# Four columns of the identity instead of 128 behind a strided operand, and one step more for reloaded inputs

## The chip, the cores and the metric

The kernel runs on one core of one Trainium2 chip. The metric is the device time of one execution in microseconds (us). The kernel before took 3438.81 us (median of 3 runs, 3435.35 to 3440.09); with the run made beside the change it is 3437.78 us (4 runs).

## The reference

A graph attention layer with 8 frames of 2048 nodes, 256 channels and 8 heads of 32, a feed-forward of 256, and three layer norms. All is float32. What matters here is the softmax over masked scores and its denominator.

```
qkv = einsum('fnc,ck->fnk', x, w_qkv)
scores = einsum('fnhd,fmhd->fhnm', q, k) / sqrt(D)
scores = where(adj > 0, scores, -1e9)
attn = softmax(scores)                      # exp / sum of exp
t = einsum('fhnm,fmhd->fnhd', attn, v)
x = layernorm(x + t); h = relu(x @ w1 + b1); x = layernorm(x + h @ w2 + b2)
return layernorm(x_in + x)
```

## The kernel before

The work is a list of 1024 steps: frame f (8), a chunk of 512 queries qc (4), a group g of four heads (2), a block of 128 keys mb (16). A step holds the scores of four heads (line 215, TensorE), the mask (line 218, VectorE, out of PSUM), the exponential (line 222, ScalarE) and the products with the values (line 234, TensorE). At most one bank of side work (projections, feed-forward, turned inputs, sums of exponentials) is put into each step, by generators that say at each `yield` what they wait for: a number of steps, or a bank.

The sums of exponentials of one group, 64 times in all:

```python
def denominator(f, qc, g):
    ...
    for n, term in enumerate(terms):          # sums over keys: ones.T @ term, heads at rows 0,32,64,96
        ...
            nc.tensor.matmul(ps[r:r + D, :], cst["ones"], term[:, h, :], ...)      # L292
    dT = op.tile([P, CH], F32, name="dT")
    nc.scalar.copy(dT, ps)                    # L294: 128 rows (32 equal ones a head) x 512 queries
    yield 1
    yield BANK
    ps = bank()
    for j in range(TPC):                      # four transposes, queries j, j+4, j+8, ...
        nc.tensor.transpose(ps[:, j * P:(j + 1) * P], dT[:, j::TPC], ident)        # L299
    ...
    den = ps.rearrange("p (j c) -> p j c", c=P)[:, :, ::D]      # one of 32 equal columns a head
    nc.vector.reciprocal(rc[:, :, 4 * g:4 * g + 4], den)                           # L304
    nc.vector.tensor_tensor(RS[:, 0], RS[:, 0], den, ALU.add)                      # L305
    nc.vector.tensor_tensor(RS[:, 1], RS[:, 1], den, ALU.min)                      # L306
```

The transposes make 128 columns of which four are read. The load of inputs that were turned before:

```python
def reload(f, c):
    ...
    xT = take([P, 2, CH], F32)
    nc.sync.dma_start(xT, XD[f][c])           # in<-xd
    yield 3                                   # steps until the first product may stand
    return xT

# in the main loop, when a step needs a projection that isn't there yet:
    while (nf, nmb // TPC, ng) not in V:
        advance(t0, 1)                        # runs side work now, and counts steps that don't pass
        t0 += 1
```

## Time and profile before

| | before |
|---|---|
| time, median | 3437.78 us |
| TensorE busy, waiting for VectorE | 3179.1 us, 174.6 us |
| VectorE, ScalarE, GpSimd busy | 2731.0, 2426.5, 2586.7 us |
| sums of exponentials (L299): records, block | 256 loads and 256 moves, 0.68 us |
| mean granted clock | 0.990 |

"Block" is the time from the first start of L299 to the start of the next work of TensorE, read from the starts of single instructions; the timeline shows the same. PE is the matrix products of TensorE and PEld the loads of their stationary operands. The prediction shows the lines and reads them.

### The profile page before, as it was taken

The page shows a single profiled execution, that of the slowest core. Times are in us where ns is not written, and L with a number is a line of the kernel's source. Part 1 is how long each engine was busy: PE and PEld are TensorE (multiplying, and loading weights), DVE is VectorE, ACT ScalarE, POOL GpSimd, SP SyncE. Part 2 cuts the span into 40 slices and gives each one's busy share as a digit, 9 for nine tenths or more (in the row PEclk, how much of TensorE's full clock was granted, in tenths as well). Part 3 has the DMA queues.
Part 4 walks back from the last instruction along what each step waited for, and adds up shares of the span by engine and source line. Part 5 has one row for each costly group of instructions (what it writes and reads, how often), then busy time and mean ns, then how long its engine had stood idle before and what let it go on. Part 6 is the DMA issues. An engine that isn't in the chain of part 4 may idle for free. (4 is left out here: it accounts for less than half of the span.)

```text
span 3439.1 us, 54435 instructions
## 1 busy us (share of the span) xinstructions
PE 3179.1 (92%) x22036; PEld 1038.5 (30%) x22036; DVE 2731.0 (79%) x3203; ACT 2426.5 (71%) x1937; POOL 2586.7 (75%) x1357
## 2 busy tenths in 40 slices
PE   6989999999999999999999999999999999998995
PEld 5222332223322233222332323223332223322222
DVE  4788768887788877888788887888768887689885
ACT  3677767776677767777677776777767777677774
POOL 0577768887688776888678876787777877788885
PEclk8999999999999999999999999999999999999998
DMA  8678768778678777778777777687776787777774
GB/s 309 149 156 173 173 161 174 158 159 200 142 167 184 154 180 153 163 172 181 170 154 170 161 175 178 141 180 172 164 179 140 160 187 167 169 158 154 151 162 99
DMA packets 149298, 575.99 MB, mean 167 GB/s; under 512 B 14608, under 2 KB 67344, under 8 KB 99888
## 3 DMA queue, kind: packets, MB, share of 16 engines
q0 software_dynamic: 64560, 435.85, 63.2%
q1 hardware_dynamic: 83664, 135.30, 11.4%
q8 instruction: 174, 2.85, 0.3%
q10 hardware_dynamic: 816, 1.31, 0.1%
q14 instruction: 84, 0.69, 0.1%
HBM read 131.99 MB, written 37.75 MB: 49 GB/s over the span
## 5 line engine op out<-in xcount | busy, mean ns | idle before, releaser
L218 DVE TENSOR_TENSOR p<-s,mask 128x1024 f32<-128x1024 f32 x2048 | 2410.0, 1219 | 568.5 <-PE s L215 343.9
L222 ACT ACTIVATE p<-p 128x2048 f32<-128x2048 f32 x1024 | 1956.6, 1911 | 484.6 <-DVE p L218 371.2
L256 POOL TENSOR_TENSOR p<-p 128x2048 f32<-128x2048 f32 x382 | 1851.8, 4898 | 385.9 <-ACT p L222 383.4
L215 PE MATMUL s<-qT,kT 32*128 32x512 f32 x8192 | 1169.8, 641 | 184.9 <-DVE p L218 174.6
L234 PE MATMUL x<-p,v 128*32 128x512 f32 x8192 | 1091.8, 605 | 2.3 <-ACT p L222 2.3
L253 POOL DMA_DIRECT2D p<-p x384 | 385.6, 1024 | 376.0 <-DMA p<-p 188.4
L215 PEld LDWEIGHTS s<-qT,kT 32*128 32x128 f32 x8192 | 320.5, 183 | 822.3 <-DVE p L218 756.2
L234 PEld LDWEIGHTS x<-p,v 128*32 128x32 f32 x8192 | 161.1, 108 | 780.1 <-issue 211.5
L172 PE MATMUL x<-in,wqkv 128*128 128x512 f32 x472 | 235.2, 621 | 14.7 <-DMA in<-xd 14.1
L292 PE MATMUL x<-p,ones 128*32 128x512 f32 x2064 | 244.9, 592 | 1.9 <-DMA p<-p 1.9
L274 ACT ACTIVATE y<-y,nb,rs 128x256 f32<-128x256 f32 x372 | 219.0, 590 | 7.1 <-POOL nb L271 7.1
L263 DVE BATCH_NORM_STATS2 st<-y 128x6 f32<-128x256 f32 x372 | 155.4, 418 | 0.0
L172 PEld LDWEIGHTS x<-in,wqkv 128*128 128x128 f32 x472 | 80.2, 189 | 170.9 <-issue 112.7
L294 ACT COPY dT<-x 128x512 f32<-128x512 f32 x64 | 37.4, 585 | 126.3 <-PE x L292 126.3
L415 PE MATMUL x<-w2s,hT 128*128 128x256 f32 x504 | 125.5, 392 | 0.1
L405 PE MATMUL x<-turned,w1s 128*128 128x512 f32 x248 | 123.0, 618 | 0.0
L197 PEld LDWEIGHTS x<-wqkv,in 128*128 128x128 f32 x896 | 104.2, 191 | 47.0 <-issue 41.1
L197 PE MATMUL x<-wqkv,in 128*128 128x128 f32 x896 | 114.9, 281 | 0.0
L292 PEld LDWEIGHTS x<-p,ones 128*32 128x32 f32 x2064 | 66.8, 110 | 156.4 <-issue 151.0
L415 PEld LDWEIGHTS x<-w2s,hT 128*128 128x128 f32 x504 | 90.6, 189 | 62.0 <-issue 50.3
L268 POOL TENSOR_TENSOR rs<-rs,mhalf 128x4 f32<-128x4 f32 x93 | 96.2, 1035 | 7.8
L200 ACT COPY v<-x 128x512 f32<-128x512 f32 x58 | 33.9, 585 | 93.6 <-PE x L197 93.6
(114 smaller groups left out, 1467.6 us busy)
## 6 DMA issues: line engine op xcount, KB each, us to landing
p<-p POOLq DMA_DIRECT2D x384, 1024.0 KB, 10.1
mask<-md SPq DMA_DIRECT2D x248, 128.0 KB, 6.2
y<-in_x_dram POOLq DMA_DIRECT2D x62, 512.0 KB, 6.1
in<-xd SPq DMA_DIRECT2D x59, 512.0 KB, 10.9
p<-in_adj_dram SPq DMA_DIRECT2D x16, 1024.0 KB, 9.6
out_dram<-y SPq DMA_DIRECT2D x31, 512.0 KB, 6.4
in<-in_x_dram SPq DMA_DIRECT2D x29, 512.0 KB, 10.4
xd<-in SPq DMA_DIRECT2D x28, 512.0 KB, 9.2
```

Source lines behind the costliest of these rows:

```text
L172: nc.tensor.matmul(ps, wqkv[:, a, k0:k0 + P], xT[:, a, :], start=(a == 0), stop=(a == 1))
L197: nc.tensor.matmul(ps[:, j * P:(j + 1) * P], xT[:, a, j * P:(j + 1) * P], wqkv[:, a, 2 * C + g * P:2 * C + (g + 1) * P], start=(a == 0), s ...
L215: nc.tensor.matmul(ps2[half][:, j, :], KT[f, mb // TPC, g][r:r + D, (mb % TPC) * P:(mb % TPC + 1) * P], QT[f, qc, g][r:r + D, :], start=Tr ...
L218: nc.vector.tensor_tensor(pt[:, 2 * half:2 * half + 2, :], ps, MK[f, qc, mb // 2][:, mb % 2, None, :].to_broadcast([P, 2, CH]), ALU.add)
L222: nc.scalar.activation(PT[item], PT[item], AF.Exp, scale=1.0 / math.sqrt(D))
L234: nc.tensor.matmul(O[grp][r:r + D, :], V[f, mb // TPC, g][:, mb % TPC, r:r + D], PT[item][:, h, :], start=(mb == 0), stop=(mb == LAST))
L253: nc.gpsimd.dma_start(PT[f, qc, g, chain[0]], PT.pop(item), accum_op=ALU.add)
L256: nc.gpsimd.tensor_tensor(first, first, PT.pop(item), ALU.add)
L263: nc.vector.bn_stats(st, t[:, j, :])
L274: nc.scalar.activation(t[:, j, :], t[:, j, :], AF.Identity, bias=nb[:, j:j + 1], scale=rs[:, j:j + 1])
L292: nc.tensor.matmul(ps[r:r + D, :], cst["ones"], term[:, h, :], start=(n == 0), stop=(n == len(terms) - 1))
L415: nc.tensor.matmul(ps[:, (j - jj) * C:(j - jj + 1) * C], hT[:, d, j * P:(j + 1) * P], w2s[:, d, :], start=(d == 0), stop=(d == 1))
```

## The change

Of each transpose's 128 columns only four are used. The change makes them alone: a true product with four columns of the identity (0, 32, 64, 96) as the moving operand, in the hope of a shorter block on the busiest engine. The second part lets the first product with a reloaded input stand one step later, in the hope that its load has landed by then.

```diff
         nc.sync.dma_start(xT, XD[f][c])
-        yield 3
+        yield 4
         return xT
...
-            nc.tensor.transpose(ps[:, j * P:(j + 1) * P], dT[:, j::TPC], ident)
+            nc.tensor.matmul(ps[:, 4 * j:4 * j + 4], dT[:, j::TPC], ident[:, ::D], start=True, stop=True)
...
-        den = ps.rearrange("p (j c) -> p j c", c=P)[:, :, ::D]
+        den = ps[:, 0:4 * TPC].rearrange("p (j h) -> p j h", h=4)
```

## The prediction

> **What bounds the kernel now.** I read the page first (busy times, the 40 slices), then the waits of TensorE, then the timeline around single sums of exponentials (the page calls them L299), then the durations line by line.
>
> The page's busy times, and the granted clock over the span:
>
> ```profile
> PE 3179.1 (92%) x22036; PEld 1038.5 (30%) x22036; DVE 2731.0 (79%) x3203; ACT 2426.5 (71%) x1937; POOL 2586.7 (75%) x1357
> ...
> PEclk8999999999999999999999999999999999999998
> ```
>
> TensorE is busy 92% at a full clock, the others 71 to 79%. The waits of TensorE say how much is left to it:
>
> ```profile
> PE s L215 <- DVE p L218: 174.6, 359, 1.5
> PE x L172 <- DMA in<-xd: 14.1, 8, 3.1
> ```
>
> Only 174.6 us of 3439 go to waiting until VectorE has freed a score bank, and 14.1 us in 8 waits to the loads of turned inputs. So TensorE bounds most steps, and VectorE the rest. There are 1024 steps. In each, the scores take 1.07 us of TensorE (start of L215 to start of L234 in the timeline below), the values 1.00, and a step may hold one bank of side work: 0.59 to 1.98. VectorE needs 2.36 us a step for the mask alone, plus its own side work. A step with no side work or a short one is VectorE's, one with a long one (1.9 us) is TensorE's. One sum of exponentials, in the timeline:
>
> ```profile
> 1450.55 1.06 PE L234 MATMUL x<-p,v 128*32 128x512 f32 x8
> 1450.74 2.35 DVE L218 TENSOR_TENSOR p<-s,mask 128x1024 f32<-128x1024 f32 x2 [0.86 <-PE s L215]
> 1451.54 0.56 PEld L299 LDWEIGHTS x<-ident,dT 128*128 128x128 f32 x4 [0.84 <-issue]
> 1451.54 0.75 PE L299 MATMUL x<-ident,dT 128*128 128x128 f32 x4
> 1452.22 0.31 PEld L215 LDWEIGHTS s<-qT,kT 32*128 32x128 f32 x8
> 1452.22 1.14 PE L215 MATMUL s<-qT,kT 32*128 32x512 f32 x8
> ...
> 1453.56 0.23 DVE L304 RECIPROCAL rc<-x 128x16 f32<-128x16 f32 x1
> ...
> 1453.73 0.16 DVE L306 TENSOR_TENSOR RS<-RS,x 128x16 f32<-128x16 f32 x1
> 1453.81 2.35 DVE L218 TENSOR_TENSOR p<-s,mask 128x1024 f32<-128x1024 f32 x2
> ```
>
> The reader is to see two things. The four transposes hold TensorE from 1451.54 to 1452.22, 0.68 us. And VectorE has no idle time from 1450.74 on (no bracket of its own after that): the scores it uses at 1453.81 ended at 1452.22 + 1.14 = 1453.36, so TensorE has a margin of 0.45 us in this step.
>
> [...] a float32 product is two records (L215 has 8192 for 4096 calls)[...]. A float32 transpose is one record (L299: 256 for 64 x 4 calls). [...] Below, a plain load takes 186 ns for 128 columns and 80 for 2: a slope of 0.84 ns a column[...] on some 79 ns of latency. [...] The transposed operand here has a step of exactly 16 bytes (every fourth float32), and its loads take 213 ns against 141 for the same transpose with contiguous operands (L394). [...] The only products of one column here (L741) start 27 ns apart (0.19 us for two records of at most 165 ns).
>
> **The change part by part.** The diff replaces a transpose by a true product with four moving columns. The columns fall from 128 to 4, but what is loaded, dT in 128 strided columns, stays, and a product is two records where a transpose was one. So each block goes from 4 loads and 4 moves to 8 loads and 8 moves. The durations by line (min/median/max in ns):
>
> ```profile
> L299 PEld LDWEIGHTS x<-ident,dT x252: 195/213/221, 159.0 to 3352.5; 128*128 128x128 f32 x126
> L299 PE MATMUL x<-ident,dT x252: 283/286/386, 159.0 to 3352.6; 128*128 128x128 f32 x126
> ```
> ```profile
> L394 PEld LDWEIGHTS x<-ident,y x256: 137/141/230, 265.9 to 3406.4; 128*128 128x128 f32 x128
> ```
> ```profile
> L197 PEld LDWEIGHTS x<-wqkv,in x896: 186/192/192, 312.2 to 3010.6; 128*128 128x128 f32 x180
> ```
> ```profile
> L741 PEld LDWEIGHTS okp<-ones,ok x2: 80/82/83, 3412.3 to 3412.3; 128*2 128x2 f32 x2
> L741 PE MATMUL okp<-ones,ok x2: 163/164/165, 3412.3 to 3412.3; 128*2 128x1 f32 x2
> ```
>
> Now: four transposes, whose starts in the trace are 0.22, 0.12 and 0.12 us apart, then 0.21 until the next block starts: 0.68. In the trace a move starts 109 ns after its load where operands are contiguous (L197, 128 columns) and 120 where they are strided (L299), and the next load starts only then. So in L197, one record each 112 ns, the move's own 107 ns hide behind the load already; taking them away gains nothing. After: about 0.11 to the first move, 7 more at 0.12 each, and 0.10 from the last move to the next block (the 0.21 of now less 0.107 of streaming): 0.11 + 0.84 + 0.10 = 1.05 us. The block gets **0.37 us longer** (an estimate from these starts), times 64 = 24 us of TensorE.
>
> How much of it reaches the end? I listed, for each of the 64 sums, TensorE's waits in the steps after it while VectorE is busy without a gap. In 16 sums of the second group a bank of 0.79 us of waiting follows, after two of 0.11: nothing gets through. In 7 others, 0.11 + 0.11 + 0.20: nothing. In 7, 0.22 in all, then a long side block: 0.15 each, 1.1 us. In 19 of the first group 0.34 (two turned blocks): 0.03 each, 0.6 us. In 4 of the last frame over 0.7: nothing. In 9 of the first group a projection of 1.9 us follows at once, and no wait for 20 us or more: all of it, 9 x 0.37 = 3.3 us. The two left, the first frame's and the very last, which stands in the chain to the end: 0.7. Sum: **5.7 us**.
>
> VectorE's part is the same work: 16 elements from contiguous instead of strided places, in 0.23, 0.11 and 0.16 us.
>
> The second part, one step more between a load of turned inputs and its first product: the order of instructions differs in one place only, six query products near 104 us, each one step later. No load waits there; the 8 waits of 14.1 us are later, in projections that are forced when scores need them, and the order leaves those alone. So it is worth nothing: 0 +- 1 us.
>
> **The rivals.** *A: fewer columns, less time.* If a load hid behind other work, a record would cost the 27 ns of L741, 8 x 0.027 + 0.2 = 0.4 us a block, 0.27 less. Against it: L741 loads 2 columns, not 128, and the pace of L197. And the same waits that hide a loss hide a gain: only some 9 to 18 sums would give it, 3 to 5 us: 3434. *B: strided plain loads at half speed.* Strided transposes load in about 98 ns (start of first to start of second load) against 56 contiguous. If plain loads doubled likewise, from 107 to 200 or more, the block would be 8 x 0.21 + 0.2 = 1.9 us, 1.2 longer, over VectorE's margin of 0.45: about 0.75 x 64 = 48 us at the end: 3487. For it: no plain strided load exists in this trace. Against it: a plain load takes only one column per 0.84 ns, and a strided transpose load reads one per 0.9 (115 ns over 126 columns), so the memory gives what a plain load needs. *C: VectorE or the loads become the bound.* Nothing of theirs changes, the order of DMA issues is the same.
>
> **Range and chances.** 3438.8 + 5.7 = 3444.5, said as 3445. My main case (some 78%) covers 3440 to 3450 with the scatter of the runs before (3435 to 3440); A (8%) gives 3432 to 3437; B (14%) 3460 to 3490. The range, 8 in 10: 3437 to 3462. Over 2% means below 3371 or above 3509: TensorE's whole 64 blocks are 64 x 0.68 = 44 us, 1.3%, so faster is all but out; slower needs B without any hiding (77 us).
>
> **What would show it.** 512 moves and 512 loads on L299 in place of 256; starts of its moves about 0.12 us apart; 1.05 us from its start to the next block; the loads at 190 to 215 ns; the waits of TensorE for VectorE down by about 18 us of their 174.6; the reload waits still 8 and about 14 us. Wrong if the records come closer than 0.1 us (A), or at 0.2 (B), or if the reload waits go.

The 107 ns that the prediction takes for a move of 128 columns is an estimate from the starts in the trace of before: records of 512 columns (L172, L405) follow each other in 429 ns, of which 107 is a quarter, and records of 256 (L415) in 216, so some 0.83 ns a column. The 3, 13, 53 and 107 ns of streaming in the expectations below are the same estimate for 4, 16, 64 and 128 columns.

## The result

The changed kernel took 3537.06 us (median of 4, 3534.58 to 3542.05), 99 us more. The ratio is 1.0291 (95% interval 1.0273 to 1.0309). Ratios here are the mean time of one kernel's fast runs over that of the other's of the same rounds, so not quite the ratio of the medians. The prediction's range ended at 3462.

The page of the changed kernel, its waits of TensorE, and the durations of its L299:

```profile
PE 3305.2 (93%) x22292; PEld 1135.7 (32%) x22292; DVE 2745.6 (78%) x3203; ACT 2428.3 (69%) x1937; POOL 2588.0 (73%) x1357
```
```profile
PE s L215 <- DVE p L218: 160.5, 355, 1.4
...
PE x L172 <- DMA in<-xd: 10.4, 6, 2.6
```
```profile
L299 PEld LDWEIGHTS x<-ident,dT x504: 307/329/332, 157.9 to 3451.4; 128*128 128x128 f32 x168
L299 PE MATMUL x<-ident,dT x504: 374/374/397, 157.9 to 3451.4; 128*128 128x4 f32 x168
```

All the other engines do the same work; TensorE has 256 products and 256 loads more, as predicted. But a load takes 329 ns, where I expected 190 to 215. The timeline of one sum, the same one that the prediction shows of before, with the step that follows:

```profile
1486.63 1.06 PE L234 MATMUL x<-p,v 128*32 128x512 f32 x8
1486.82 2.36 DVE L218 TENSOR_TENSOR p<-s,mask 128x1024 f32<-128x1024 f32 x2 [0.86 <-PE s L215]
1487.62 1.94 PEld L299 LDWEIGHTS x<-ident,dT 128*128 128x128 f32 x8 [0.84 <-issue]
...
1489.59 1.97 PE L215 MATMUL s<-qT,kT 32*128 32x512 f32 x8
...
1491.48 1.88 PE L234 MATMUL x<-p,v 128*32 128x512 f32 x8
...
1491.60 2.35 DVE L218 TENSOR_TENSOR p<-s,mask 128x1024 f32<-128x1024 f32 x2 [1.55 <-PE s L215]
...
1493.98 1.14 PE L215 MATMUL s<-qT,kT 32*128 32x512 f32 x8
```

Two things are to be seen. The block runs from 1487.62 to 1489.59, **1.96 us** where it was 0.68 (all but the last of the 64 blocks have this length). And the scores and values right after it take 1.97 and 1.88 us, where before, and again at 1493.98, they take 1.14 and 1.06. The busy times by stretch (length, then busy time and count of PE, PEld, DVE, ACT, POOL, the granted clock, DMA) say why:

```profile
1486.40:1489.80 3.40, 3.40 (x24) 2.32 (x24) 2.94 (x5) 2.22 (x2) 1.00 (x2) 1.00 0.94 193
1489.80:1493.20 3.40, 3.40 (x16) 0.38 (x12) 1.85 (x5) 1.38 (x1) 3.13 (x5) 0.50 0.95 193
1493.20:1496.60 3.40, 3.40 (x28) 1.59 (x24) 2.86 (x4) 1.91 (x1) 3.01 (x1) 1.00 1.11 231
```

For one window of 3.41 us the granted clock is 0.50. PE is "busy" for all of each stretch; only the clock tells. The page's 40 slices of 88 us do not show such windows, their digit stays 9. The mean over the whole run does, and is the first thing I should have looked at in the result; here before and after:

```profile
core 0: 3439.1 us, clock 0.990
```
```profile
core 0: 3537.2 us, clock 0.974
```

From the clock's records between the first sum and the end I counted the halved windows that begin within 4 us of a block's start: 35 of the 64 blocks in the changed kernel, none of before. (The long halved stretches near the end, 7 us and more, which every kernel here has, are left out, here and below.) Each of the 35 is 3.41 us long, and they lie on a grid of 3.41 us. All blocks that start 0.13 to 1.34 us after a grid line (32), or at most 0.08 us before one (3), have the clock halved in the next window; of the 29 that start elsewhere none has. Those 35 are the blocks whose loads, some 1.9 us long, lie inside one window, wholly or but for the first 0.08 us.

**Where the 99 us lie.** The order of the steps is the same, so I compared the start of the k-th scores in both traces. Across each of the 29 sums without a halved window the kernel falls back by 0.90 us on average; across each of the 35 with one, by 2.07. That is 64 x 0.90 = 58 us for the longer blocks and 35 x 1.17 = 41 us for the clock, 99 in all. This is bookkeeping on one pair of traces; the experiments test it.

### The profile page after: what moved, and what is told of

The parts are those of the page before. It is cut to its first block, busy times and chain, and to the rows that moved or that the text cites. A ratio compares the mean times of both kernels' runs of the same rounds, so it can differ in the third digit from the quotient of the medians.

```text
span 3537.2 us, 54947 instructions
## 1 busy us (share of the span) xinstructions
PE 3305.2 (93%) x22292; PEld 1135.7 (32%) x22292; DVE 2745.6 (78%) x3203; ACT 2428.3 (69%) x1937; POOL 2588.0 (73%) x1357
## 4 chain that ended last, share of the span: by engine, by line
PE 72%; DVE 15%; DMA 4%; issue 4%; POOL 2%; ACT 1%; DVEq 0%; SPq 0%; ACTq 0%; POOLq 0%
PE s L215 27%; PE x L234 17%; DVE p L218 14%; PE x L292 6%; PE x L172 6%; PE x L299 3%; PE x L415 3%; PE x L405 3%; PE x L197 3%; DMA in<-xd 2%; DMA p<-p 1%; PE x L394 1%; PE x L152 1%; DMA xd<-in 1%; POOL p L256 1%
## 5 line engine op out<-in xcount | busy, mean ns | idle before, releaser
L215 PE MATMUL s<-qT,kT 32*128 32x512 f32 x8192 | 1185.7, 649 | 163.1 <-DVE p L218 160.5
L234 PE MATMUL x<-p,v 128*32 128x512 f32 x8192 | 1120.4, 620 | 1.5 <-ACT p L222 1.5
L172 PE MATMUL x<-in,wqkv 128*128 128x512 f32 x472 | 235.3, 621 | 10.4 <-DMA in<-xd 10.4
L299 PEld LDWEIGHTS x<-ident,dT 128*128 128x128 f32 x504 | 122.4, 327 | 52.8 <-issue 52.8
L172 PEld LDWEIGHTS x<-in,wqkv 128*128 128x128 f32 x472 | 80.6, 190 | 169.2 <-issue 112.4
L299 PE MATMUL x<-ident,dT 128*128 128x4 f32 x504 | 127.9, 377 | 0.0
L415 PE MATMUL x<-w2s,hT 128*128 128x256 f32 x504 | 125.5, 392 | 0.3 <-DVE y L417 0.3
L405 PE MATMUL x<-turned,w1s 128*128 128x512 f32 x248 | 123.0, 618 | 0.0
L197 PEld LDWEIGHTS x<-wqkv,in 128*128 128x128 f32 x896 | 104.2, 191 | 47.0 <-issue 41.1
L197 PE MATMUL x<-wqkv,in 128*128 128x128 f32 x896 | 114.9, 281 | 0.0
L415 PEld LDWEIGHTS x<-w2s,hT 128*128 128x128 f32 x504 | 90.6, 189 | 62.2 <-issue 50.3
```

Of the source, the lines that this page charges most:

```text
L172: nc.tensor.matmul(ps, wqkv[:, a, k0:k0 + P], xT[:, a, :], start=(a == 0), stop=(a == 1))
L197: nc.tensor.matmul(ps[:, j * P:(j + 1) * P], xT[:, a, j * P:(j + 1) * P], wqkv[:, a, 2 * C + g * P:2 * C + (g + 1) * P], start=(a == 0), s ...
L215: nc.tensor.matmul(ps2[half][:, j, :], KT[f, mb // TPC, g][r:r + D, (mb % TPC) * P:(mb % TPC + 1) * P], QT[f, qc, g][r:r + D, :], start=Tr ...
L234: nc.tensor.matmul(O[grp][r:r + D, :], V[f, mb // TPC, g][:, mb % TPC, r:r + D], PT[item][:, h, :], start=(mb == 0), stop=(mb == LAST))
L299: nc.tensor.matmul(ps[:, 4 * j:4 * j + 4], dT[:, j::TPC], ident[:, ::D], start=True, stop=True)
L405: nc.tensor.matmul(ps, w1s[:, a, d * P:(d + 1) * P], yT[:, a, :], start=(a == 0), stop=(a == 1))
```

## The experiments

My theory, to be tested: the product's stationary operand loads in 329 ns because its elements lie four float32 apart, where a contiguous one of the same shape (L197) takes 192 (some 58 us); and the clock is halved in the window after one that holds such a block because little is streamed there (some 41 us). Rivals: the halved windows cost nothing; the clock falls for another reason; the later step matters.

### The two parts alone

```diff
-        yield 3
+        yield 4
```

> The transposes stay; only the wait of a load of turned inputs becomes one step longer. Theory (the whole loss comes from the product): 3438 us, within 3 us of before, ratio 0.999 to 1.001, no half-clock window besides the one near 2518 us. Rival (the later first product costs something of its own, or the shifted phase of the loads does): a ratio above 1.003, over 10 us.

Measured: ratio 0.9996 (0.9986 to 1.0005), no half-clock window tied to a sum. I had expected only the halved window that before has near 2519 us, just after a wait of 3.1 us for a reloaded input; here there are two others, near 440 and 2102 us, after such waits of 2.6 and 2.7 us. The later step alone is worth nothing.

The other part alone is the change with `yield 3` kept.

> The product with four columns in place of the transposes, the loads' wait as before. Theory: all of the loss, 3537 us (ratio 1.026 to 1.032), 1.96 us from the start of a block of L299 to the next block, some 30 to 38 half-clock windows of 3.41 us. Rival (part of the loss is the later step's): clearly under 3530.

Measured: 3548.66 us against 3447.29 beside it, ratio 1.0295 (1.0275 to 1.0315), block 1.96 us, 34 blocks with a halved window. (This chip and session is some 10 us slower for the kernel before, too; so only ratios are compared.) All of the loss is the product's.

### More columns behind the same loads

```diff
-            nc.tensor.matmul(ps[:, 4 * j:4 * j + 4], dT[:, j::TPC], ident[:, ::D], ...)
+            nc.tensor.matmul(ps[:, j * P:(j + 1) * P], dT[:, j::TPC], ident, ...)
```

> The same strided product, but it moves all 128 columns of the identity: the loads stay, the array streams 107 ns of each 233 instead of 3. Two-part theory (load time plus a clock that halves after a stretch of little streaming): the block becomes about 2.07 us (a last move of 107 ns is added), the half-clock windows go to 0 to 3, and the time falls to about 3500 (before plus 64 x 1.0). Rival (all of the loss is load time, the half-clock windows cost nothing because VectorE waits hide them): no gain, 3540 to 3545. Second rival (the clock halves for loads or strides as such, not for little streaming): some 35 windows stay and the time is 3540 or more.

Measured: ratio 1.0193 (1.0171 to 1.0215), some 66 us over before. The durations, and the clock of the run:

```profile
L299 PEld LDWEIGHTS x<-ident,dT x504: 307/329/332, 161.4 to 3425.4; 128*128 128x128 f32 x168
L299 PE MATMUL x<-ident,dT x504: 397/397/500, 161.5 to 3425.5; 128*128 128x128 f32 x168
```
```profile
core 0: 3512.6 us, clock 0.988
```

The loads are the same to the nanosecond and the block is even longer (2.06 us), yet the kernel is faster than with four columns, and no halved window is tied to a block. Five lie elsewhere before the last sum (I had expected at most 3 in all); each begins within 1.1 us of the end of a wait of 2.3 to 2.9 us for a reloaded input. Moving 32 times as many columns is faster by a whole percent. That refutes both rivals in this kernel: without the halved windows the time is shorter (1.0193 against 1.0295 for the product with four columns), and the same strided loads of 329 ns stand in 64 blocks of which none has one.

The same with 64 columns (`ident[:, ::2]`):

> The strided product moving 64 columns: 53 ns of streaming in each 233 (23%). Window theory: a window with a whole block in it has 1.45 us of other work and 0.23 x 1.96 us of streaming[...]: no half-clock window tied to a block, block about 2.0 us, ratio about 1.018 like all columns. Rival (the clock halves for moves of fewer than some 100 columns, whatever the share): some 35 windows, ratio 1.028 or more.

Measured: ratio 1.0169 (1.0151 to 1.0186), block 2.01 us, no halved window tied to a block. Against e2_product_only (1.0295) that is 0.0126 of 3440, some **43 us for the clock** (give or take 9 by the two intervals), and 58 us remain for the longer blocks; the two sums of the traces were 41 and 58. And with 16 columns (`ident[:, ::8]`):

> The strided product moving 16 columns: 13 ns of streaming in each 233, 6% of the block. In the changed kernel a block halves the clock only where all of some 1.9 us of it lies in one window of 3.41[...]. Window theory[...]: no half-clock window tied to a block, ratio about 1.017, as with 64 columns. Rival (few columns as such[...]): some 20 to 35 windows tied to blocks, ratio 1.024 or more.

Measured: ratio 1.023 (1.0209 to 1.0252), 17 blocks with a halved window of 3.41 us, each falling back by 2.14 us on average, the other 47 by 1.08. I had expected none, from an estimate of my own of how much a window has to stream; it missed, and where the limit lies was not shown. The 17 blocks, about a quarter of all and half as many as with four columns, start from 0.01 us before to 0.33 after a grid line or 0.98 to 1.24 after one; 13 blocks that start in between (0.39 to 0.97) lie in one window too and have no halved window after them. What else in the window decides was not shown.

### Contiguous loads

The copy to dT sorts the queries, so that the four operands are contiguous:

```diff
-        nc.scalar.copy(dT, ps)
+        nc.scalar.copy(dT.rearrange("p (j q) -> p j q", j=TPC), ps.rearrange("p (q j) -> p j q", j=TPC))
-            ... dT[:, j::TPC], ident[:, ::D] ...
+            ... dT[:, j * P:(j + 1) * P], ident[:, ::D] ...
```

> The product with four columns, but the copy to dT by ScalarE sorts the queries, so that the loaded operand is contiguous. Two-part theory, with the stride as the cause of the long loads: starts of the moves 0.11 us apart as in L197, the block about 1.05 us, which was my prediction's main case: 3443 us (3440 to 3450), and no half-clock windows[...]. Rival (plain loads cost 233 ns in front of a short move whatever the stride): block 1.96, time 3530 or more. Rival on the clock (it falls after any run of short moves): block 1.05 but tens of half-clock windows and 3470 or more.

Measured: ratio 1.0039 (1.0025 to 1.0053), 13 us over before.

```profile
L299 PEld LDWEIGHTS x<-ident,dT x504: 186/192/192, 161.8 to 3379.6; 128*128 128x128 f32 x168
L299 PE MATMUL x<-ident,dT x504: 252/253/273, 161.8 to 3379.7; 128*128 128x4 f32 x168
```

Same product, same four columns: 192 ns a load instead of 329, moves 0.112 us apart instead of 0.233, block 0.99 us, no halved window tied to a block. So the stride is the cause of the long loads here. This is also my prediction's main case made real, and it costs 13 us, not 6. In its profile (at 3469 us the slowest of its nine runs) the reload waits are 20.7 us (14.1 before), and ten halved windows, in eight places, lie between the first sum and the last, none tied to a sum (before: one). At each place TensorE waits 2 to 3.5 us just before or in the window: five times for a reloaded input, twice for VectorE, once for ScalarE. Compared with before by the starts of the scores, as above, the kernel falls back by 0.055 us on average in the few steps after a sum, 3.5 us in all; most of the 26 us that this profile falls back lies at those waits and windows. So in this one trace the blocks cost about what my list of 5.7 us gave them, and the loss beyond it is in waits for other work and the clock after them. What moved those waits was not tested.

Steps of 8 bytes instead of 16, with the sums at other queries (relative error 0.13). Its output is wrong, which doesn't matter for the time.

```diff
-            ... dT[:, j::TPC] ...
+            ... dT[:, (j // 2) * 2 * P + j % 2:(j // 2) * 2 * P + 2 * P:2] ...
```

> Wrong result on purpose: the product loads every second float32 (step of 8 bytes) instead of every fourth (16 bytes); the sums land at other queries, the work is the same. Theory[...]: loads as fast as contiguous ones, moves 0.11 us apart, block 0.99 us as in the contiguous run, ratio 1.002 to 1.006. Rival (any step slows a plain load): moves clearly more than 0.13 us apart, block over 1.2 us, ratio above 1.008.

Measured: ratio 1.0034 (1.0022 to 1.0046).

```profile
L299 PEld LDWEIGHTS x<-ident,dT x504: 192/196/198, 160.9 to 3362.0; 128*128 128x128 f32 x168
```

Loads of 196 ns, moves 0.118 us apart, block 1.04 us: 5% more than contiguous. A step of two float32 adds 4 ns to a load here, the step of four 137.

### The same loads in two halves

```diff
-        yield BANK
-        ps = bank()
-        for j in range(TPC): ... four products; three VectorE instructions on 16 columns
+        for half in (slice(0, 2), slice(2, 4)):
+            yield BANK
+            ps = bank()
+            for j in range(TPC)[half]: ... two products; three VectorE instructions on 8 columns
```

> The strided product with four columns as in the change, in two banks of two columns blocks each, one step of scores and values between them. Same loads, same streaming. Window theory[...]: no half-clock window tied to these blocks, since at most 1.3 us of loading falls into one window. Time: before plus 64 x (1.3 longer plus about 0.2 for the second start and three more small VectorE instructions, of which some 1.0 gets through): 3500 to 3520, ratio 1.016 to 1.024. Rival (short moves as such halve the clock): as many windows, ratio over 1.03.

Measured: ratio 1.0056 (1.0041 to 1.0071), 19 us over before. With the same 512 strided loads and four columns, no half-clock window is left in the steady part (the only two after the start lie in the last 45 us). So short moves alone do not halve the clock in this kernel: the same products in halves of 1.03 us, with a step of scores and values in between, leave none of the 34 or 35 halved windows that follow blocks of 1.96 us. But it was far faster than I expected, so my sum of the blocks did not fit this case. The control with transposes:

> The control of the two halves: the same two banks, order and step as in e8_two_halves, with transposes in place of products, so that only the loads differ. Theory (the long loads cost less there because half a block of 1.05 us mostly fits into what VectorE leaves, and the rest is the extra bank and six small VectorE instructions): ratio 1.000 to 1.003, so the products' loads cost 10 to 20 us of the 19 measured. Rival (the extra bank itself is the cost of e8_two_halves): 1.004 to 1.006, as there.

Measured: 3434.74 us against 3449.43, ratio **0.9959** (0.9944 to 0.9974): faster than before, which neither theory had. The reload waits, 14.1 us before, are gone from its list of waits (and from e8_two_halves'), and so is the halved window near 2519 us. Its longest waits of TensorE:

```profile
PE s L215 <- DVE p L218: 171.5, 374, 1.4
PE s L126 <- DVE p L483: 12.5, 6, 3.1
PE s L152 <- DMA p<-in_x_dram: 7.7, 1, 7.7
PE x L395 <- ACT y L367: 6.7, 2, 5.4
PE x L126 <- DVE p L483: 5.8, 3, 2.0
```

So the long loads in halves cost 1.0056 - 0.9959, some 33 us, instead of 58: half a block is 1.03 us against 0.44 for two transposes (where no wait follows them), 0.59 longer, and VectorE's margin of about 0.45 in such a step would hide part of that; I did not trace it step by step, so this is argued, not shown. The halves with their extra step, but without the long loads, gain 14 us. To see whether the shift alone does it, one step per sum was left empty, with the four transposes in one block:

```diff
         yield BANK
+        yield BANK
         ps = bank()
```

> The kernel before with one step left free of side work ahead of the transposes of each sum: it shifts the side work one step later as the transposes in halves do, without halving anything. Theory (transposes in halves were 0.4% faster because the shift gives the reloaded inputs a step more and their waits of 14 us go): the reload waits vanish here too, ratio 0.995 to 0.998. Rival (the gain came from halves that fit into what VectorE leaves): reload waits as before or not, ratio 0.999 to 1.003.

Measured: ratio 0.9976 (0.9965 to 0.9986), reload waits 8.1 us in 5. So part of the gain, some 8 of 14 us, comes with the shift alone. The traces, one of each kernel, show what became of the waits: none of before's eight is left at its step in either kernel, but the spare step has new ones at other steps, four of them 1.9 to 2.2 us long, and the halves have none. Why the halves have none was not tested. The total of these waits does not set the time by itself: e1_step_only has 10.3 us of them and e10_sorted_copies (below) 9.4, and neither gains anything clear of noise.

### Sorted copies, alone and with the halves

> A try to beat both: transposes as before, but the two copies of ScalarE (dT and oT) sort the queries, so that all these transposes load contiguous operands. Theory: blocks of L299 and L328 go from 0.68 to 0.59 us; before them VectorE bounds the steps with L328, so only the first group's sums and the steps that TensorE bounds gain: 64 x 0.09 at most 6 us, likely 1 to 3: ratio 0.999 to 1.000, within noise. Rival (the copies with a strided read take longer on ScalarE): copies over 0.65 us and a ratio above 1.001.

The edits are those of the contiguous product on both copies, with transposes. Measured: ratio 0.9995 (0.9987 to 1.0004); transposes load in 140 instead of 213 ns, the block of L299 is 0.59 us, and the copies take 0.585 us as before. TensorE's gain turns into waiting for VectorE: 186.2 us instead of 174.6.

> A try to beat both kernels by more: transposes in halves, with both copies sorting the queries so that these transposes load contiguous operands. Theory: the gain of the halves (ratio 0.996) and that of the sorted copies (0.9995) add up: 0.994 to 0.997, with half blocks of about 0.37 us instead of 0.44. Rival: VectorE bounds those steps and nothing is added: 0.996 to 0.997.

Measured: 3432.22 us against 3444.97, ratio 0.9963 (0.9949 to 0.9976). It beats both kernels, like the halves alone, and isn't distinguished from them.

## Why the prediction was wrong

- **The bound, right.** TensorE in long steps, VectorE in short ones; a longer block showed as less waiting for VectorE (174.6 to 160.5 us; I said down by 18).
- **Two records for a product, eight loads a block, right** (512 of each).
- **The length of the block, wrong: 1.05 us predicted, 1.96 measured. This is the step that failed first.** I had noted that strided transposes load in 98 ns against 56 (from the first load of a block to the second; the medians of the contiguous L152 and L394 are 57 and 59; later ones follow in 0.12 us against 0.11), and that one strided load takes 213 ns against 141. Then I took the pace of the contiguous product (L197, 0.112) over to the strided one, because "a plain load takes only one column per 0.84 ns, and a strided transpose load reads one per 0.9 (...), so the memory gives what a plain load needs". That 0.9 fits the shortest load of L299, 195 ns; its median of 213 gives 1.06, and both are above 0.84. Measured, the strided product's load takes (329 - 80)/126, some 2.0 ns a column. The runs show the factor carries over instead: starts of loads are 0.109 to 0.112 us apart contiguous and 0.213 to 0.233 strided. Rival B said exactly this, 1.9 us; I gave it 14%.
- **What gets through, right in kind, a little small.** For B I took 0.75 us of 1.2 per sum, from VectorE's margin of 0.45. Without halved windows the traces show 0.90 of 1.28. For a block 0.36 us longer the step-two run falls back by 0.11 a sum in its profile, 7 us, where my list gave 5.7 for 0.37; the 12 us it lost in time contain more than that.
- **The clock, missing.** The prediction has no term for it. I read that the clock was 9 in all slices but the first and the last and took it as given, and I treated the moves' 107 ns as free to take away. Without them the clock was halved after 35 of the 64 blocks, with 64 or 128 columns after none: 41 us by the traces, 43 by the 64-column run.
- **The second part, right: nothing.** The order of instructions showed it: the 8 waits belong to projections that are forced in the loop, where steps are only counted. But to conclude that these waits can't be had would be wrong: the halves removed them. And I said that they would stay 8 and about 14 us: the changed kernel has 6 of 10.4 us, the step alone 7 of 10.3, at no gain in time.
- **The chances.** "Slower needs B without any hiding" failed for want of the clock: B with hiding, 58 us, plus 41.

## What to carry to other kernels

In a stream of small products, count the loads and how they read memory before the moved columns. Here a product of four columns had two loads of 329 ns where a transpose of 128 had one of 213, and a block took 1.96 us instead of 0.68. Fewer columns behind the same loads saved 0.10 us a block (1.96 against 2.06), and the kernel was slower for it (1.0295 against 1.0193). Look at the step of a float32 stationary operand: a load took 192 ns contiguous, 196 at a step of two and 329 at a step of four. After a change to TensorE, look at the mean granted clock first (0.990 before, 0.974 after): here a block that mostly loaded was paid for again in the window after it in 35 of 64 cases, at 1.17 us each.
